# Four graph-attention layers: rows spread over the partitions by BF16 products of three parts, in place of FP32 transposes of a broadcast column

## The chip, the cores and the metric

The kernel runs on one core of a Trainium2 chip. The metric is the device time of one execution in microseconds; the figure for a kernel is the median of its runs. One further execution is taken by the hardware profiler, and all views of the profile come from that one.

## What is computed

The input `x` has 32 graphs of 512 nodes with 256 features; one adjacency matrix `adj` of 512 x 512 serves all of them. Each graph goes through four layers, each of them `x = x + gnn(relu(layernorm(x)), adj)`. The attention of a layer has this core (here layer 2; the others differ in the slope, in the mask and in the closing function):

```python
Wh = jnp.einsum('bnf,fo->bno', h, W)
s_i = Wh @ a1
s_j = Wh @ a2
e = leaky_relu(s_i[:, :, None] + s_j[:, None, :], negative_slope=0.2)
e = jnp.where(mask[None, :, :], e, -inf)
attention = softmax(e, axis=-1)
h_prime = jnp.einsum('bij,bjo->bio', attention, Wh)
return elu(h_prime)
```

Layer 0 does this with four heads of 64 features. Layer 1 has two attentions with dense layers around them: one over all pairs of nodes, with no mask and 512 features, and one with the mask. Layers 2 and 3 have one head of 256 features.

## The kernel before, in words

**Tiling.** A graph's 512 nodes lie as four tiles of 128 partitions (`NT` = 4). The loop at the end of `gat_stack` runs over the 32 graphs, called batches here, and records for each the pieces of all four layers: layer norm and transposition (`layernorm_relu_T`), products with the weights (`project`, `dense_relu_T`), attention (`gat_heads`, `full_gat_T`, `gat`), and the closing functions (`add_elu` and its like). Products are FP32 with 128 x 128 weights (`product`, L408).

**Rows.** The scores e are the sum of one number per row and one per column. A number per node comes as a column, one per partition. To add it along the free axis it must be a row, the same in all 128 partitions. The kernel makes such rows in two ways:

- `spread` (L621) makes a row of 512 in PSUM: for each of the four node tiles it broadcasts the column of 128 numbers to 128 x 128 and transposes it on TensorE in FP32 (`transposes`, L398). In the profile these are the instructions `row<-ident,...`.
- `lines` and `row_of` (L627, L641) transpose the column, copy it to SBUF, write it to DRAM as a line and read it back into all partitions by DMA (`line<-turned`, `rb<-line`).

`spread` is called 15 times per batch. `peaks` (L647) needs one row for each of the four heads and each of the three single-head attentions; from it VectorE takes the largest masked score of each node (`left`, L654). `weights_T` (L683) needs one for each of the same seven; with it VectorE makes `y` (L697), to which GpSimd adds the mask (L707, L715) and of which ScalarE takes the exponential into `pt` (L708, L722), the weights of the last product. `full_gat_T` (L827) needs one, for `ptf` (L877). The row of `tmax` in the same function is made by a transpose of its own, not by `spread`. Between the peaks and the weights, `score_columns` (L667) computes the columns u, top, ca, cb, cc, ct by tiny instructions on VectorE and GpSimd.

**Order.** Nothing is issued where it is recorded. `do` (`Plan.add`) stores each piece with its engine, a price in ns, its inputs and outputs. `Plan.order` then runs a list scheduler over all batches: up to `DEPTH` = 5 batches are open at a time, and on each engine the ready piece with the lowest key goes first. The key is the batch's number times `PERIOD` (103600 ns) minus a due time from a list: `FIRST` for the setup, `URGENCY` for a batch, the same list for each. The resulting order is fixed in the program: every engine issues its pieces in that order, and the hardware's semaphores make it wait where an input is late. Tiles come from pools with a fixed number of buffers per kind (`SLOTS`), of which the scheduler keeps account.

**Filler.** Where the schedule leaves TensorE a gap of 400 ns or more, dummy transposes (`filled`, L1017) are put in: six tenths of the gap at 110 ns each (`FILL`, `FILL_NS`, `FILL_FROM`). Their result is not used.

Of the kernel before, what the change touches and what calls it, by code (L numbers as in the profile page):

```python
# [10 lines left out]
BF16 = mybir.dt.bfloat16  # L11
# [22 lines left out]
SLOTS = {"b8": (7, 3), "b4": (14, 4), "b2": (14, 4), "b1": (10, 2), "ps": (7, 0), "tiny": (1000, 0), "dram": (12, 0)}  # L34

DEPTH = 5
PERIOD = 103600
# [7 lines left out]
    49957, 66495, 153342, 82735, 144893, 18248, 163947, 104419, 59651, 169283, 167420, 27958, 91780, 230242,  # L45
    195004, 201919, 109150, 118275, 41409, 148351, 105924, 84158, 33663, 128315, -31046, 92771, 80073,
    -45028, 28235, 136777, -16929, 40188, 120535, 69018, 81157, 34057, 45864, 64938, 93847, 22979, 32782,
    -10095, -7685, 78515, -28222, 19420, -8026, 14562, 65514, 92596, 50809, 54059, 90452, -2420, 84889,
    -14583, 182093, 91531, 6874, 128004, -23771, -69759, 210945, 103417, 96629, 177264, 97081, 141216,
    228810, 79944, 208774, 181698, 34991, 127254, 226356, -9989, 145084, 102532, 51302, 57785, 135746,  # L50
    80518, 8900, 128919, 64999, 72213, 100118, -191301, 129287, 126778, 107678, 38434, 214310, -59056,
    21096, 128569, -77796, 31871, 74871, 45424, 52264, -8376, 19505, -47500, 133347, 67984, 70285, 186177,
    -15984, 104650, 146444, -6977, 74654, 209924, -4928, 74371, 174294, 40423, 51951, 50262, 29464, 45416,
    3988, 20540, -30268, 143961, 32626, 29520, 89804, -46895, -71848, 192873, -94019, -16097, 82357,
    -169645, 44440, 58074, 23239, 29426, 38323, 69931, 62358, 28167, 54402, 35577, -76917, -57030, -27704,
    46576, -51547, -24313, -49157, 37623, -166471, -262408, -40277, -75897, 2495, -34811, -74370, 10822,
    -15615, -38619, -14324, 87924, -14732, 53506, -26615, -76490, 65133, 111389, 71959, 93636, 216417,
    118024, 163785, 26618, -73110, 16741, 9419, -10974, -26368, 86308, 35587, -14529, 9505, -23652, 31209,
    -35827, 87676, 57894, 76693, 67541, -81967, -32754, 78132, 16981, 15839, 11266, -39752, -44185, -180983,
    -106465, -45466, -89834, -11687, 103426, 151973, 157389, 186709, 237443, 270307, 278957, 17921, 218966,  # L60
    105429, 178416, 116249, 84788, 142806, 50637, 86803, 147442, 126624, 122625, -24526, 224818, 181273,
    122134, 261099, 188560, 278444, 309233, 202098, 46668, 146708, 13559, -27972, -149859, 4547, -115510,
    38885, 107791, -163000, 38869, -279727, -120416, -64868, -65585, -103808, 25837, -296121, 16410, -66665,
    -247882, -82470, -195328, -56781, -67125, -74463, -260380, -10356, -293322, -28794, -66573, -118165,
    117861, -244495, 33153, -14981, 71927, -75326, 49632, -75897, 12372, -59742, -253914, -34455, -280537,
    60459, -56427, -20405, -76842, -84804, -76638, -87008, 6362, -96566, -92921, -140211, -40235, 9737,
    1430, 138501, -8164, -11585, -790, 92727, -18209, -59964, 33770, 120062, 48291, -69971, -116178, -43376,
    -75934, -22587, -855, -7366, 64764, -21815, -173536, -191622, -247, -89468, -141561, -5472, -71333,
    -71091, -23345, -35224, -60425, -31184, -36678, -96715, -93204, -104153, 122741, -103991, -49069,
    -52273, 103915, -129888, -87436, -90017, -84147, -248017, -153179, -142134, -195377, -246140, -94749,  # L70
    -281312, -209508, -156148, -170174, -173938, -110763, -202784, -90958, -123778, -230905, -217447,
    -158358, -191908, -181567, -150880, -166302, -173285, -145335, -192412, -213127, -112164, -79463,
    -80154, -45304, -115344, -213688, -61711, -71844, -179488, -7519, -10195, -123581, -92377, -130342,
    -156089, -168165, -158280, -78069, -97410, 20095, 52768, -118896, -100859, -22248, -140758, -98924,
    -171258, -214761, -144742, -191503, -188885, -161622, -179163, -210494, -197100, -75155, -143396,
    -114654, -120868, -88478, -67661, -85469, -105261, -231208, -147545, -195786, -143928, -132751, -203479,
    -51238, -198637, -307380, -218655, -234274, -292902, -81910, -227932, -110271, -9939, -267811, -133305,
    96531, -164689, -28167, 25068, -163586, -170683, -125323, -118603, -47000, -182274, -161878, -209482,
    -210149, -168999, -138546, -191158, -233690, -133535, -231298, -285256, -155744, -125493, -243944,
    -223209, -190911, -249846, -244877, -146750, -260327, -392277, -245282, -212678, -202761, -168108,  # L80
    -206988, -163184, -234077, -225292, -151778, -418885, -146975, -166246, -197351, -165479, -253278,
    -164022, -7427, -227404, -223194, -205947, -290945, -299944, -191474, -275233, -246375, -249699,
    -253455, -249835, -216585, -256193, -283065, -390887, -270743, -284915, -267017, -418553, -281245,
    -293102, -238408, -177593, -347600, -366149, -358476, -414408, -536943, -384769, -405112, -314429,
    -370595, -265928, -543033, -409858, -416969, -320333, -443009, -407966, -431291, -243310, -493060,
    -378266, -346645, -225670, -370270, -376164, -325328, -399421, -374586, -398079, -417234, -461239,
    -465521, -400816, -409787, -543463, -345783, -366473, -257474, -479888, -496847, -470513,
]
FIRST = [
    -31437, 25750, -1105, 144955, 89002, 275880, 128415, 204208, 154195, 226450, 96820, 179479, 7870,  # L90
    -118045, 26290, 146438, 138609, 157057, 205913, -16123, 59630, 57501, -56814, 5247, -4577, -6068,
    -45189, -27458, 74268, 87671, 62434, 55789, -15727, -51036, -133151, -170623, -122434, -106956, -88821,
    -45241, -84685, -17322, -151531, 663, -157813, -74980, -174232, -62374, -58576, 11927, -19486, -48352,
    77279, -175495, -146175, -169316, -241074, -142701, -178875, -141702, -62487, -96044, -41405, -94885,
    -228054, -41409, -191710, -235324, -125187, -188700, -74514, -165891, -142656, -170202, 6399, -96844,
    -155386, -142053, -171779, -291299, -271981, -405298, -401521, -247815, -210715, -198935, -245058,
    -90055, -125151, -183656, -54990, -77623, -143327, -261274, -244716, -325695, -246171,
# [224 lines left out]
def gat_stack(  # L322
# [33 lines left out]
    small = ctx.enter_context(tc.tile_pool(name="small", bufs=7))  # L356
# [7 lines left out]
    def take(t):  # L364
        if t.kind == "ps":
            t.real = ps.tile(t.shape, t.dtype, name=t.name, tag="ps")
        elif t.kind == "dram":
            t.real = dram.tile(t.shape, t.dtype, name=t.name, tag="line%d" % t.shape[0])
        elif t.kind == "tiny":
            t.real = small.tile(t.shape, t.dtype, name=t.name)  # L370
        else:
            t.real = sized(t.kind, t.name, t.shape, t.dtype)
# [21 lines left out]
    def transposes(dst, srcs, holds=()):  # L394


        def run(o, *parts):
            return [nc.tensor.transpose(o[:, n * P : (n + 1) * P], a, ident) for n, a in enumerate(parts)]  # L398

        do(PE, 109.2 * len(srcs), [dst], srcs, run, holds)  # L400
# [21 lines left out]
    make_identity(nc, ident)  # L422
    minus1 = const.tile([P, 1], F32, name="minus1")
# [197 lines left out]
    def spread(cols, holds=()):  # L621

        row = Later("ps", "row", [P, N])
        transposes(row.all, [cols(t).view(lambda a: a.to_broadcast([P, P])) for t in range(NT)], holds)
        return row
# [21 lines left out]
    def peaks(t_col, far, peak):  # L647

        row = spread(t_col)
# [33 lines left out]
    def weights_T(ca, line_b, cc, ct, farT, even):  # L683
# [5 lines left out]
        row_a = spread(ca, [pt])  # L689
# [50 lines left out]
    def gat(srcT, wx, far, farT, lift, slope, own, finish):  # L740
# [8 lines left out]
        peaks(lambda t: v[:, t, D + 2 : D + 3], far, lambda it: peak[:, it : it + 1])  # L749
# [12 lines left out]
        ca, *cs = (lambda t, c=c: c[:, t : t + 1] for c in (ca, *cs))  # L762
        pt = weights_T(ca, (line_b, 0), *cs, farT, not own)
# [12 lines left out]
    def gat_heads(srcT, wx, far, farT, slope, finish):  # L776
# [13 lines left out]
        peak = Later("tiny", "peak_h", [P, H, NT])  # L790
        for hd in range(H):
            peaks(lambda t: st[:, 1, hd, t : t + 1], far, lambda it: peak[:, hd, it : it + 1])
# [277 lines left out]
```

## Time and profile before

| what | us |
|---|---|
| median of 3 runs (3439.34 to 3440.38) | 3439.69 |
| the profiled execution's own time | 3439.76 |
| its span, first to last instruction | 3437.8 |
| TensorE busy, weight loads aside | 3397.8 |
| VectorE busy | 2629.5 |
| ScalarE busy | 1962.7 |
| GpSimd busy | 1657.1 |

The lines of the profile are read like this. A group of instructions is named by its line in the kernel, engine and operation, then output `<-` inputs by the program's tile names, the shapes and the number of instructions; after the first bar stand the time in which at least one of the group ran and the mean duration in ns; after the second, the engine's idle time just before them and what ended it. PE is TensorE, PEld its weight loads (they overlap with PE), DVE VectorE, ACT ScalarE, POOL GpSimd, SP the engine that issues the DMAs. TensorE is pipelined: one record lasts longer than the distance to the next, so durations of neighbours overlap. An FP32 product is recorded as two instructions, an FP32 transpose as one. The timeline gives the start and the length of runs of like instructions in us from the span's start.

### The profile page before, as it was taken

Reading aid. Unit: us, or ns where it says so; the run is one execution under the profiler, and the core shown is the slowest. Engines: PE = TensorE matmul, PEld = TensorE weight load, DVE = VectorE, ACT = ScalarE, POOL = GpSimd, SP = SyncE. Lnnn points to the kernel's source line nnn. Section 1 sums busy time; section 2 is a strip of 40 time slices with the busy share of each in tenths; the row PEclk is TensorE's granted clock in tenths of the full one; section 3 lists DMA queues with packets and bytes.
Section 4 is the critical chain, followed back from the end, with each engine's and each line's share of the span. In section 5 each row is a group of like instructions: output and inputs, shape, how many; then the busy total and the mean of one; then the engine's idle time right before and its main releaser. Section 6 shows DMA issues by size and latency. Waiting matters only on the chain. (4 is left out here: it accounts for less than half of the span.)

```text
span 3437.8 us, 55266 instructions
## 1 busy us (share of the span) xinstructions
PE 3397.8 (99%) x18801; PEld 2861.4 (83%) x18801; DVE 2629.5 (76%) x8200; ACT 1962.7 (57%) x4109; POOL 1657.1 (48%) x2089
## 2 busy tenths in 40 slices
PE   7999999999999999999999999999999999999998
PEld 7788888888888888888888888888888888888887
DVE  8587877777777777777777877777878777777764
ACT  4555565565655565555566655556655655655543
POOL 3253554454544454545444545544544545544544
PEclk9999999999999999999999999999999999999999
DMA  3000110011110011110010110010110011110000
GB/s 111 19 29 14 35 38 31 17 38 32 35 38 26 22 38 32 35 38 26 22 38 29 37 38 26 22 37 29 38 38 21 27 32 35 38 32 16 32 19 28
DMA packets 77978, 110.51 MB, mean 32 GB/s; under 512 B 7169, under 2 KB 43521, under 8 KB 77697
## 3 DMA queue, kind: packets, MB, share of 16 engines
q1 hardware_dynamic: 77696, 106.98, 9.9%
q8 instruction: 150, 2.46, 0.3%
q14 instruction: 132, 1.07, 0.1%
HBM read 89.66 MB, written 17.30 MB: 31 GB/s over the span
## 5 line engine op out<-in xcount | busy, mean ns | idle before, releaser
L715 POOL TENSOR_TENSOR y<-y,farT_some 128x512 f32<-128x512 f32 x512 | 584.9, 1176 | 311.1 <-DVE y L697 308.3
L408 PE MATMUL mm<-v,pt 128*128 128x257 f32 x3072 | 704.1, 380 | 7.0 <-ACT pt L708 4.2
L697 DVE SCALAR_TENSOR_TENSOR y<-row,cc,rb 128x512 f32<-128x512 f32 x896 | 625.2, 742 | 73.1 <-DMA rb<-line 53.5
L408 PEld LDWEIGHTS mm<-v,pt 128*128 128x128 f32 x3072 | 575.5, 190 | 88.4 <-ACT pt L708 5.4
L722 ACT ACTIVATE pt<-y,ct 128x512 f32<-128x512 f32 x640 | 459.3, 719 | 291.2 <-POOL y L715 271.5
L408 PEld LDWEIGHTS mmh<-vh,pt 128*128 128x128 f32 x4096 | 483.3, 192 | 10.0 <-ACT pt L722 1.8
L408 PE MATMUL mmh<-vh,pt 128*128 128x65 f32 x4096 | 481.8, 272 | 1.4 <-DVE y L697 0.6
L408 PE MATMUL mm<-hfc,ptf 128*128 128x257 f32 (+1 forms) x2048 | 465.6, 381 | 0.5 <-DVE ptf L877 0.4
L408 PE MATMUL mm<-wfc,out1T 128*128 128x257 f32 x2048 | 464.4, 379 | 0.0
L408 PEld LDWEIGHTS mm<-wfc,out1T 128*128 128x128 f32 x2048 | 382.2, 189 | 53.6
L408 PEld LDWEIGHTS mm<-hfc,ptf 128*128 128x128 f32 x2048 | 380.8, 189 | 52.7 <-issue 2.0
L654 DVE CUSTOM_DVE_ANT_0 left<-row,far_nz 128x512 bf16<-128x512 f32 x640 | 413.9, 681 | 9.1 <-PE row L398 9.1
L707 POOL TENSOR_TENSOR y<-y,g 128x512 f32<-128x512 f32 x256 | 323.1, 1274 | 93.7 <-issue 42.9
L613 ACT ACTIVATE h<-xt,shift,rstd 128x256 f32<-128x256 f32 x512 | 277.5, 592 | 32.1 <-DVE shift L605 32.0
L598 POOL TENSOR_SCALAR rstd<-mv 128x4 f32<-128x4 f32 x128 | 34.3, 268 | 533.9 <-DVE mv L1014 356.0
L939 ACT ACTIVATE ez<-mm,rden 128x256 f32<-128x256 f32 x256 | 120.8, 472 | 238.6 <-DVE rden L1014 167.1
L408 PE MATMUL mm<-hT,w 128*128 128x512 f32 x512 | 233.2, 592 | 0.0
L654 DVE CUSTOM_DVE_ANT_0 left<-row,far_pos 128x512 bf16<-128x512 f32 x256 | 165.5, 685 | 86.5 <-PE row L398 86.5
L408 PE MATMUL mm<-out1T,wm 128*128 128x512 f32 x512 | 224.9, 592 | 0.0
L708 ACT ACTIVATE pt<-y 128x512 f32<-128x512 f32 x256 | 160.6, 628 | 82.7 <-POOL y L707 82.7
L1014 DVE BATCH_NORM_STATS2 stats<-xt 128x6 f32<-128x256 f32 x512 | 196.9, 414 | 5.6 <-DMA xt<-in_x_dram 5.2
L971 POOL TENSOR_TENSOR xt<-xt,rz 128x256 f32<-128x256 f32 x128 | 100.8, 797 | 199.7 <-ACT rz L970 196.3
(150 smaller groups left out, 5636.8 us busy)
## 6 DMA issues: line engine op xcount, KB each, us to landing
rb<-line SPq DMA_DIRECT2D x256, 256.0 KB
xt<-in_x_dram SPq DMA_DIRECT2D x32, 512.0 KB
out_dram<-xt SPq DMA_DIRECT2D x32, 512.0 KB
line<-turned SPq DMA_DIRECT2D x128, 2.0 KB
adj_sb<-in_adj_dram SPq DMA_DIRECT2D x1, 1024.0 KB
wfc<-in_L_gnn_W_fc_dram SPq DMA_DIRECT2D x2, 512.0 KB
a_row<-in_L_gnn_a_dram SPq DMA_DIRECT2D x3, 256.0 KB
a_row<-in_L_gnn_a_fc_dram SPq DMA_DIRECT2D x1, 512.0 KB
```

What stands on the lines that cost most here:

```text
L408: nc.tensor.matmul(o, lhsT=parts[k], rhs=parts[nk + k], start=(k == 0), stop=(k == nk - 1))
L598: do(POOL, 200, [rstd.all], [mv[:, :, 1]], lambda o, a: nc.gpsimd.tensor_scalar(o, a, EPS, None, ALU.add))
L613: lambda o, a, m, s: nc.scalar.activation(o, a, AF.Relu, bias=m, scale=s),
L654: return nc.vector.tensor_tensor_reduce(out=junk, in0=a, in1=far, scale=1.0, scalar=LOWEST, op0=ALU.add, op1=ALU.max, accum_out=o,)
L697: lambda o, a, c, b: nc.vector.scalar_tensor_tensor(o, a, c, b, ALU.add, ALU.max),
L707: do(POOL, 1255, [y.all], [y.all, g.all], lambda o, y, g: nc.gpsimd.tensor_tensor(o, y, g, ALU.add))
L708: do(ACT, 521, [pt[:, jt, :]], [y.all], lambda o, a: nc.scalar.activation(o, a, AF.Exp))
L715: lambda o, y, far: nc.gpsimd.tensor_tensor(o, y, far, ALU.add),
L722: lambda o, a, c: nc.scalar.activation(o, a, AF.Exp, bias=c),
L939: do(ACT, ns, [o.all], [z, scale], lambda o, a, s=scale, f=f: nc.scalar.activation(o, a, f, scale=s))
L971: do(POOL, 685, [xi], [xi, r.all], lambda o, a, b: nc.gpsimd.tensor_tensor(o, a, b, ALU.add))
L1014: made = p.run(*(r.ap() if isinstance(r, Ref) else r for r in p.args))
```

## The change

The function `spread` is gone. In its place stand two. `in_parts` splits a column of FP32 numbers (or n columns at once) into three BF16 parts whose sum is the number: cast, subtract, cast, subtract on VectorE. It transposes the 3n columns with one BF16 transpose on TensorE and copies the result, 3n x 128, to SBUF on ScalarE. `sum_row` then makes the row: for each node tile a BF16 product of 128 columns, whose weights (`pick`) are ones for the three parts wanted and zeros elsewhere, broadcast to 128 columns. Its FP32 sum in every partition is the number.

`in_parts` is called nine times per batch: twice for all four heads together (48 lines), twice for each of the three single-head attentions and once in the full one (12 lines). `sum_row` is called 15 times, where `spread` was.

The setup makes a BF16 identity and the two `pick` tiles on GpSimd. The kind b1 has 8 buffers in place of 10, tiny 6 in place of 7, a new kind tb 6. `PERIOD` is 101300, and the lists `FIRST` and `URGENCY` have new numbers throughout. The rule for the filler is as before.

```diff
-SLOTS = {"b8": (7, 3), "b4": (14, 4), "b2": (14, 4), "b1": (10, 2), "ps": (7, 0), "tiny": (1000, 0), "dram": (12, 0)}
+SLOTS = {"b8": (7, 3), "b4": (14, 4), "b2": (14, 4), "b1": (8, 2), "ps": (7, 0), "tb": (6, 1), "tiny": (1000, 0), "dram": (12, 0)}
...
-PERIOD = 103600
+PERIOD = 101300
...
-    small = ctx.enter_context(tc.tile_pool(name="small", bufs=7))
+    small = ctx.enter_context(tc.tile_pool(name="small", bufs=6))
...
+    ident_b = const.tile([P, P], BF16, name="ident_b")
+    nc.gpsimd.tensor_copy(ident_b, ident)
+    picks = {}
+    for n in (NT, H * NT):
+        pick = picks[n] = const.tile([P, n], BF16, name="pick%d" % n)
+        nc.gpsimd.tensor_tensor(pick, ident[:, :n], ident[:, n : 2 * n], ALU.add)
+        nc.gpsimd.tensor_tensor(pick, pick, ident[:, 2 * n : 3 * n], ALU.add)
...
-    def spread(cols, holds=()):
-        row = Later("ps", "row", [P, N])
-        transposes(row.all, [cols(t).view(lambda a: a.to_broadcast([P, P])) for t in range(NT)], holds)
+    def in_parts(cols, n, name):
+        parts = Later("tiny", "parts", [P, 3, n], BF16)
+        rest = Later("tiny", "rest", [P, n])
+        turned = Later("tb", "turned_" + name, [3 * n, P], BF16)
+        tr = Later("ps", "trb", [3 * n, P], BF16)
+        do(DVE, 78, [parts[:, 0]], [cols], nc.vector.tensor_copy)
+        do(DVE, 78, [rest.all], [cols, parts[:, 0]], lambda o, a, b: nc.vector.tensor_tensor(o, a, b, ALU.subtract))
+        do(DVE, 78, [parts[:, 1]], [rest.all], nc.vector.tensor_copy)
+        do(
+            DVE,
+            78,
+            [parts[:, 2]],
+            [rest.all, parts[:, 1]],
+            lambda o, a, b: nc.vector.tensor_tensor(o, a, b, ALU.subtract),
+        )
+        do(
+            PE,
+            60,
+            [tr.all],
+            [parts.all.view(lambda a: a.rearrange("p x n -> p (x n)"))],
+            lambda o, a: nc.tensor.transpose(o, a, ident_b),
+        )
+        copy(ACT, turned.all, tr.all, P)
+        return turned
+
+    def sum_row(turned, first, holds=()):
+        row = Later("ps", "rowb", [P, N])
+        pick = picks[turned.shape[0] // 3]
+        def run(o, lines):
+            return [
+                nc.tensor.matmul(
+                    o[:, t * P : (t + 1) * P],
+                    lhsT=pick[: lines.shape[0], first + t : first + t + 1].to_broadcast([lines.shape[0], P]),
+                    rhs=lines,
+                    start=True,
+                    stop=True,
+                )
+                for t in range(NT)
+            ]
+        do(PE, 58 * NT, [row.all], [turned.all], run, holds)
         return row
...
-        row = spread(t_col)
+        row = sum_row(parts, first)
...
-        row_a = spread(ca, [pt])
+        row_a = sum_row(parts_a, first, [pt])
...
-        peaks(lambda t: v[:, t, D + 2 : D + 3], far, lambda it: peak[:, it : it + 1])
+        peaks(in_parts(v[:, :, D + 2], NT, "t"), 0, far, lambda it: peak[:, it : it + 1])
...
-        pt = weights_T(ca, (line_b, 0), *cs, farT, not own)
+        pt = weights_T(in_parts(ca.all, NT, "a"), 0, (line_b, 0), *cs, farT, not own)
...
+        parts_t = in_parts(st[:, 1].view(lambda a: a.rearrange("p h t -> p (h t)")), H * NT, "th")
         for hd in range(H):
-            peaks(lambda t: st[:, 1, hd, t : t + 1], far, lambda it: peak[:, hd, it : it + 1])
+            peaks(parts_t, hd * NT, far, lambda it: peak[:, hd, it : it + 1])
...
+        parts_a = in_parts(flat[0], H * NT, "ah")
         for hd in range(H):
-            ch, *cs_h = (lambda t, c=c: c[:, hd, t : t + 1] for c in (ca, *cs))
-            pt = weights_T(ch, (line_b, hd), *cs_h, farT, False)
+            cs_h = (lambda t, c=c: c[:, hd, t : t + 1] for c in cs)
+            pt = weights_T(parts_a, hd * NT, (line_b, hd), *cs_h, farT, False)
...
-        q_row = spread(lambda t: c[:, 1, t : t + 1], [pt])
+        q_row = sum_row(in_parts(c[:, 1, :], NT, "q"), 0, [pt])
```

## The prediction

> **What bounds the kernel now.** I read the page's busy table first, then the table by stretches of time, then the groups of instructions and the timeline of TensorE, to learn what one spread of a row costs.
>
> ```profile
> span 3437.8 us, 55266 instructions
> ...
> PE 3397.8 (99%) x18801; PEld 2861.4 (83%) x18801; DVE 2629.5 (76%) x8200; ACT 1962.7 (57%) x4109; POOL 1657.1 (48%) x2089
> ```
>
> A busy share is an average, so the middle of the run is asked alone (columns: stretch, its length, busy us and instructions of PE, PEld, DVE, ACT, POOL, then clock and DMA):
>
> ```profile
> 1500.00:2500.00 1000.00, 999.49 (x5528) 845.10 (x5527) 779.73 (x2456) 587.82 (x1235) 496.05 (x621) 1.00 0.10 32
> ```
>
> TensorE lacks half a microsecond of 1000 at full clock; VectorE has 22% free, ScalarE 41%, GpSimd 50%. Busy here could still be filler[...]. The same table for the tile "filled" (PE, then PEld) says it is not:
>
> ```profile
> 0.00:100.00 100.00, 23.08 (x192) 21.70 (x192) 0.95 0.32 106
> 100.00:300.00 200.00, 0.00 (x0) 0.00 (x0) 1.00 0.06 19
> 300.00:3200.00 2900.00, 0.38 (x2) 0.25 (x2) 1.00 0.10 31
> 3200.00:3438.00 238.00, 36.02 (x303) 33.88 (x303) 0.99 0.07 21
> ```
>
> So the middle is pure TensorE work, and a batch costs what its TensorE instructions cost. The transposition of tmax comes once a batch, and two in a row show the period:
>
> ```profile
> 2033.39 0.27 PE L398 MATMUL row<-ident,tmax 128*128 128x128 f32 x1
> ...
> 2137.14 0.27 PE L398 MATMUL row<-ident,tmax 128*128 128x128 f32 x1
> ```
>
> 2137.14 - 2033.39 = 103.75 us per batch. Only the start and the end have idle time and filler. The removed instructions are these, by the groups:
>
> ```profile
> L398 PE MATMUL row<-ident,ca 128*128 128x128 f32 x896 | 132.0, 277 | 0.6 <-DVE ca L677 0.5
> ...
> L398 PE MATMUL row<-ident,st 128*128 128x128 f32 x512 | 66.6, 273 | 0.0
> ...
> L398 PE MATMUL row<-ident,v 128*128 128x128 f32 x384 | 58.3, 273 | 0.0
> ...
> L398 PE MATMUL row<-ident,c 128*128 128x128 f32 x128 | 19.2, 273 | 0.0
> ```
>
> The mean of 273 ns is latency, in which neighbours overlap; the cost is the distance from start to start:
>
> ```profile
> 613.65 1.00 PE L408 MATMUL mmh<-vh,pt 128*128 128x65 f32 x8
> 614.49 0.60 PE L398 MATMUL row<-ident,ca 128*128 128x128 f32 x4
> 614.93 1.90 PE L408 MATMUL mmh<-vh,pt 128*128 128x65 f32 x16
> 616.66 0.60 PE L398 MATMUL tr<-ident,ef 128*128 128x128 f32 x4
> ```
>
> Four transposes take 614.93 - 614.49 = 0.44 us. Over all spread records between 400 and 3200 us, start to start is 109.2 ns. The mmh products, which stream only 65 columns, still take about 0.11 us a record (1.73 us for 16)[...].
>
> [...] No instruction of the kernel before is a BF16 product[...]. [...] the same tiny subtraction ca takes 155 ns in the median and 464 ns in the mean, 1262 at most.
>
> **The change, part by part.**
>
> Removed: per batch (896 + 512 + 384 + 128) / 32 = 60 transposes of 109.2 ns, 6.55 us of TensorE, all on the path in the middle.
>
> Added on TensorE: 60 BF16 products of 128 columns, each with a weight load of its own, and 9 BF16 transposes (two for the four heads, two for each of three single-head layers, one for the full layer). [...] I take 58[...], since in this trace loads run wholly behind the products and a BF16 column is half as wide. A transpose loads only 12 or 48 columns and streams 128[...], and I take 60. Sum: 60 x 0.058 + 9 x 0.060 = 3.48 + 0.54 = 4.02 us. Saved: 6.55 - 4.02 = 2.53 us a batch, 81 us in 32.
>
> Added on VectorE: 9 x 4 = 36 tiny instructions a batch: 18 casts at some 155 ns and 18 subtractions of two SBUF inputs at 155 to 464 ns: 2.8 + 2.8 to 8.4 = 5.6 to 11.2 us. VectorE now works 0.780 x 103.75 = 80.9 us a batch and would work 86.5 to 92.1 of about 101.2. That costs nothing while this is hidden beside TensorE; if the order leaves no slack at some place, TensorE waits. Queued behind a late subtraction are VectorE's y, left and PSUM copies, and those feed GpSimd, ScalarE and then the products. I allow 0.1 us a batch, 3 us in all (below nothing is excluded: TensorE had no stall to lose).
>
> Added on ScalarE: 9 copies of the turned parts at 239 ns, 2.2 us, on 61.0 us of work: hidden. Its queue has them ahead of exps by a quarter of a microsecond each.
>
> The chain from a column to its row grows by four dependent VectorE steps of 0.2 us (u to top to cb at the end of the trace are 0.2 us apart), a transpose of 0.27 and a copy of 0.26 us, some 1.5 us with the handovers. In the middle other batches cover it. For the second rows (from ca) the DMA path through lines and row_of is longer anyway (line and rb take 1.15 and 2.98 us at the end of the trace). For the first rows (peaks) there is no such cover at the start and the end.
>
> Start and end: before, 497 fillers of 109 ns (54 us) and 3437.8 - 3397.8 = 40 us of idle, of which 10 precede the first instruction: 84 us that go with the fillers. The built order of the changed kernel has 584 fillers, 251 at the start and 333 at the end, none between. The rule that sets them, a fixed share of each long gap, is unchanged, so I scale: 84 x 584 / 497 = 99, +15 us. Bounds: 0 (the new order's gaps are only cut up differently) to 25.
>
> Moved or shrunk: PERIOD and the lists alter the order only; SP's 128 line and 256 rb transfers, and the loads and stores, are as many as before and DMA is at 10%. Fewer b1 and tiny buffers could make a VectorE write wait for an old reader; they are short-lived, so nothing, and what they may cost lies within the stall case below. Five small GpSimd instructions at setup fall into the 9.86 us in which TensorE waits for data anyway.
>
> Sum on the profiled execution (3439.76 us: the span of 3437.8 and 2.0 around it; the median is 3439.69, the same): 3439.8 - 81 + 15 + 3 = 3377 us.
>
> **Rivals.**
>
> Stalls: VectorE at 86 to 91% with long dependent chains of tiny steps lets TensorE wait about 1 us a batch, 32 us in all in place of 3: 3406. For it: the long waits on GpSimd; against: TensorE lost 0.5 us of 1000 with VectorE at 78%.
>
> [...]
>
> Slower: the new weight loads on TensorE run at the FP32 pace, so a product takes 111 ns, the change doesn't do what it says, and the nine transposes come on top: 60 x 1.8 ns + 0.54 = 0.65 us a batch, 21 us, plus 15: 3476. It decides from a product of 109.2 - 9 (transposes, 0.54 / 60) - 8 (15 us / 32 / 60) = 92 ns on. For it: mmh's pace; against: a cast to 16 bits halves the bytes of each column[...].
>
> **Chances.** The forecast (3350 to 3395) 0.68, stalls 0.12[...], slower 0.08, a time within the 0.2% (7 us, about what a measurement of this kernel tells from no change; a product near 92 ns) 0.02. So faster 0.90, same 0.02, slower 0.08. The low end takes [...] no longer start or end: 3439.8 - 87 = 3353, so 3352. The high end takes in stalls [...]: 3424. What is left out is the slower end and the tails, under 2 in 10.
>
> **What would show it.** Start to start of rowb products about 58 ns, under 0.24 us for a row of four; a period of about 101.2 us; VectorE at 86 to 91% in the middle and TensorE still above 99.5%; fillers none in the middle. Wrong if rowb pairs take 80 ns or more, if TensorE in the middle waits for parts, turned or y, or if start and end take over 25 us more.

## The result and the profile after

| | before | changed |
|---|---|---|
| median of 6 runs, us | 3439.52 | 3535.92 |
| lowest to highest | 3437.66 to 3440.85 | 3533.04 to 3537.91 |
| profiled span | 3437.8 | 3535.3 |

The ratio is 1.028, with a 95% interval from 1.0267 to 1.0294: the change makes the kernel slower by 96 us, where 63 us of gain were forecast. The profile's busy table:

```profile
span 3535.3 us, 57262 instructions
...
PE 3497.4 (99%) x19176; PEld 2762.5 (78%) x19176; DVE 2792.9 (79%) x9352; ACT 2063.2 (58%) x4397; POOL 1635.9 (46%) x2094
```

Its table by stretches, in the middle of the run:

```profile
1500.00:2500.00 1000.00, 999.63 (x5413) 782.52 (x5412) 799.47 (x2721) 598.37 (x1279) 469.23 (x609) 1.00 0.10 30
```

TensorE still counts as busy for all but 0.4 us of 1000 and the clock is full, and VectorE is at 80%, less than the forecast's 86 to 91%. So it looks as before: bound by TensorE, with no stall. The fillers, too, are at the start and the end (the 25 of the third stretch lie before 500 us):

```profile
0.00:100.00 100.00, 28.09 (x206) 24.41 (x206) 0.98 0.32 106
100.00:300.00 200.00, 2.79 (x20) 2.19 (x20) 1.00 0.06 20
300.00:3300.00 3000.00, 3.49 (x25) 2.78 (x25) 1.00 0.10 30
3300.00:3536.00 236.00, 41.94 (x333) 36.50 (x333) 0.99 0.07 21
```

Yet the period, from one tmax transposition to the next in the timeline, is longer:

```profile
2094.32 0.27 PE L404 MATMUL row<-ident,tmax 128*128 128x128 f32 x1
2201.01 0.27 PE L404 MATMUL row<-ident,tmax 128*128 128x128 f32 x1
```

2201.01 - 2094.32 = 106.69 us in place of 103.75 (the median of all periods is 106.70). 32 x 2.95 = 94 us; the rest of the span, the span less 32 periods, grew only from 117.7 to 121.1 us. All of the loss is in the steady middle, on an engine that never seems to wait. The groups that answer to the removed transposes:

```profile
L670 PE MATMUL rowb<-turned_ah,pick 48*128 48x128 bf16 x512 | 48.6, 218 | 0.8
...
L657 PE MATMUL trb<-ident_b,parts 128*12 128x128 bf16 x224 | 44.8, 221 | 2.5 <-DVE parts L650 2.1
...
L670 PE MATMUL rowb<-turned_th,pick 48*128 48x128 bf16 x512 | 40.1, 218 | 2.7 <-DVE y L753 2.7
...
L670 PE MATMUL rowb<-turned_a,pick 12*128 12x128 bf16 x384 | 37.7, 217 | 0.0
L670 PE MATMUL rowb<-turned_t,pick 12*128 12x128 bf16 x384 | 37.7, 217 | 0.1
```

(The numbers ahead of the shape are the rows and columns of the array in use.) Their latencies of 217 to 221 ns, below the 273 of the transposes before, show nothing wrong. The timeline of TensorE shows what the averages hide:

```profile
1008.16 1.03 PE L414 MATMUL mm<-wfc,out1T 128*128 128x257 f32 x4
1009.13 0.39 PE L670 MATMUL rowb<-turned_a,pick 12*128 12x128 bf16 x4
1009.45 2.00 PE L414 MATMUL mm<-wfc,out1T 128*128 128x257 f32 x8
1011.38 0.39 PE L670 MATMUL rowb<-turned_a,pick 12*128 12x128 bf16 x4
1011.71 0.24 PE L657 MATMUL trb<-ident_b,parts 128*48 128x128 bf16 x1
```

Eight FP32 records of 217 ns should take 1.74 us from 1009.45 on; the next row starts at 1011.38, 1.93 us later. The row's four products should take 0.22 us; the next FP32 product starts after 0.32. And the weight loads (PEld), which elsewhere start a whole product early (in the kernel before, between `mm<-hfc,ptf` products, the loads of a row start at 606.07 us and its first transpose at 606.29, one FP32 record of 0.22 us later):

```profile
1009.12 0.22 PEld L670 LDWEIGHTS <-pick 12*128 12x128 bf16 x4 [0.33 <-issue]
1009.45 1.60 PEld L414 LDWEIGHTS mm<-wfc,out1T 128*128 128x128 f32 x8
```

Both begin together with the product that needs them: at each border nothing is loaded ahead, and PEld stood idle for 0.33 us just before the row's loads. Over the middle of the run, medians from start to start: the last FP32 product before a row takes 310 ns in place of 216, the last BF16 one 145 in place of 56, and the first FP32 record behind it 321 in place of 216 (a transpose 165 in place of 109). That is some 94 + 89 + 105 = 288 ns for each visit to the new instructions, and a batch has 18 visits.

### The profile page after: what moved, and what is told of

Read it like the earlier page. It is cut to its first block, busy times and chain, and to the rows that moved or that the text cites. A ratio compares the mean times of both kernels' runs of the same rounds, so it can differ in the third digit from the quotient of the medians.

```text
span 3535.3 us, 57262 instructions
## 1 busy us (share of the span) xinstructions
PE 3497.4 (99%) x19176; PEld 2762.5 (78%) x19176; DVE 2792.9 (79%) x9352; ACT 2063.2 (58%) x4397; POOL 1635.9 (46%) x2094
## 4 chain that ended last, share of the span: by engine, by line
PE 94%; DVE 4%; DMA 1%; ACT 1%; POOL 0%; issue 0%; POOLq 0%; DVEq 0%; ACTq 0%; SPq 0%
PE mm L414 70%; PE mmh L414 12%; PE tr L404 6%; PE rowb L670 4%; PE trb L657 1%; DVE y L753 1%; DVE left L710 1%; PE tr L688 1%; DVE stats L1073 0%; DMA rb<-line 0%; PE filled L1076 0%; DVE parts L1073 0%; DVE xt L1008 0%; DVE ez L1007 0%; POOL y L763 0%
## 5 line engine op out<-in xcount | busy, mean ns | idle before, releaser
L753 DVE SCALAR_TENSOR_TENSOR y<-rowb,cc,rb 128x512 f32<-128x512 f32 x896 | 625.8, 738 | 20.4 <-PE rowb L670 8.4
L414 PE MATMUL mm<-wfc,out1T 128*128 128x257 f32 x2048 | 483.9, 385 | 0.0
L414 PEld LDWEIGHTS mmh<-vh,pt 128*128 128x128 f32 x4096 | 475.3, 192 | 9.6 <-ACT pt L778 0.9
L710 DVE CUSTOM_DVE_ANT_0 left<-rowb,far_nz 128x512 bf16<-128x512 f32 x640 | 413.8, 679 | 9.9 <-PE rowb L670 9.7
L1019 POOL TENSOR_TENSOR rz<-rz,res 128x256 f32<-128x256 f32 x128 | 98.2, 767 | 336.2 <-ACT rz L998 278.0
L771 POOL TENSOR_TENSOR y<-y,farT_self 128x512 f32<-128x512 f32 x128 | 145.4, 1159 | 227.2 <-DVE y L753 227.2
L414 PE MATMUL mm<-hT,w 128*128 128x512 f32 x512 | 241.2, 605 | 0.0
L1073 DVE BATCH_NORM_STATS2 stats<-xt 128x6 f32<-128x256 f32 x512 | 205.3, 412 | 5.6 <-DMA xt<-in_x_dram 4.3
L670 PEld LDWEIGHTS <-pick 48*128 48x128 bf16 (+1 forms) x1920 | 107.6, 93 | 126.7 <-issue 91.9
L710 DVE CUSTOM_DVE_ANT_0 left<-rowb,far_pos 128x512 bf16<-128x512 f32 x256 | 168.0, 683 | 48.9 <-PE rowb L670 48.8
```

What stands on the lines that cost most here:

```text
L414: nc.tensor.matmul(o, lhsT=parts[k], rhs=parts[nk + k], start=(k == 0), stop=(k == nk - 1))
L670: nc.tensor.matmul(o[:, t * P : (t + 1) * P], lhsT=pick[: lines.shape[0], first + t : first + t + 1].to_broadcast([lines.shape[0], P]), rh ...
L710: return nc.vector.tensor_tensor_reduce(out=junk, in0=a, in1=far, scale=1.0, scalar=LOWEST, op0=ALU.add, op1=ALU.max, accum_out=o,)
L753: lambda o, a, c, b: nc.vector.scalar_tensor_tensor(o, a, c, b, ALU.add, ALU.max),
L771: lambda o, y, far: nc.gpsimd.tensor_tensor(o, y, far, ALU.add),
L1019: do(POOL, 685, [r], [r, res[:, it, :]], lambda o, a, b: nc.gpsimd.tensor_tensor(o, a, b, ALU.add))
```

## The experiments

The theories, as they stood at the first runs. S: each change of TensorE from FP32 to BF16 and back costs this. R: not the type but the number of rows or columns of the array in use does. V: the visit is a symptom, and the added VectorE and ScalarE work, the longer chains or the new order cost the time.

**Pairs of instructions alone** (e1_pairs). No part of the kernel is used; TensorE gets rounds of a stretch A and a stretch B, for instance:

```diff
+        ("f_bfull", f128, 4, b128s, 4),
+        ("f_btwelve", f128, 4, b12s, 4),
...
+        ("f_ftwelve", f128, 4, f12s, 4),
+        ("f_fturn", f128, 4, t12, 1),
...
+        ("b_btwelve", b128, 8, b12s, 4),
...
+        for r in range(REPS):
+            for k in range(na):
+                a(oa, k)
+            for k in range(nb):
+                b(ob, k)
```

> The kernel leaves the whole computation out: it copies x to the output and issues sections of TensorE instructions alone, each 24 times: a stretch A (8 FP32 records of 256 columns, or 8 FP32 transposes, or 8 BF16 products), then a stretch B (4 or 16 BF16 or FP32 products of 128 columns with 12, 48 or 128 rows, or one transpose of 12 columns). Read is the time of a round over what its parts stream. Theory S (each change of TensorE from FP32 to BF16 and back lays the weight load bare): about 0.29 us a round for FP32 products with BF16 behind them, whether of 12 or 128 rows, 4 or 16 of them, or a BF16 transpose; 0.24 us where A are FP32 transposes; nothing where both are FP32 (12 rows, or a transpose of 12 columns) and nothing where both are BF16. Rival R (the change of the number of rows or columns in use does it): about 0.29 us for FP32 with FP32 of 12 rows and for BF16 with BF16 of 12 or 48 rows, nothing for FP32 with BF16 of 128 rows.

```profile
211.18 1.95 PE L46 MATMUL f_bfull_A<-xt 128*128 128x256 f32 x8
212.96 0.39 PE L46 MATMUL f_bfull_B<-xb 128*128 128x128 bf16 x4
213.18 1.51 PE L46 MATMUL f_bfull_A<-xt 128*128 128x256 f32 x6
...
262.23 1.99 PE L46 MATMUL f_btwelve_A<-xt 128*128 128x256 f32 x8
264.16 0.39 PE L46 MATMUL f_btwelve_B<-xb 12*128 12x128 bf16 x4
264.48 0.70 PE L46 MATMUL f_btwelve_A<-xt 128*128 128x256 f32 x2
...
457.16 0.27 PE L70 MATMUL f_fturn_B<-ident,xt 128*12 128x128 f32 x1
457.27 1.03 PE L46 MATMUL f_fturn_A<-xt 128*128 128x256 f32 x4
...
621.06 1.05 PE L46 MATMUL b_btwelve_A<-xb 128*128 128x256 bf16 x8
622.04 0.39 PE L46 MATMUL b_btwelve_B<-xb 12*128 12x128 bf16 x4
622.36 0.83 PE L46 MATMUL b_btwelve_A<-xb 128*128 128x256 bf16 x6
```

With all 128 rows (bfull) the row's four products take 213.18 - 212.96 = 0.22 us, as they stream; with 12 rows (btwelve) 0.32, the same 0.1 us too long as in the kernel. Median rounds, less what the parts stream (216 ns for an FP32 record of 256 columns, 109 for a BF16 product of 256 columns or an FP32 transpose, 56 for a BF16 product or transpose of 128, and for the FP32 products of B, two records of 128 columns each, the pace inside their stretch, 112 a record with few rows and 109 with few columns):

| A | B | round, ns | streams, ns | extra, ns |
|---|---|---|---|---|
| FP32 products | 4 BF16, 128 rows | 2006 | 1952 | 54 |
| FP32 products | 4 BF16, 12 rows | 2249 | 1952 | 297 |
| FP32 products | 16 BF16, 12 rows | 2919 | 2624 | 295 |
| FP32 transposes | 4 BF16, 12 rows | 1347 | 1096 | 251 |
| FP32 products | 4 FP32, 12 rows | 3007 | 2624 | 383 |
| FP32 products | 1 FP32 transpose, 12 columns | 1838 | 1837 | 1 |
| FP32 products | 1 BF16 transpose, 12 columns | 2076 | 1784 | 292 |
| BF16 products | 4 BF16, 128 rows | 1097 | 1096 | 1 |
| BF16 products | 4 BF16, 12 rows | 1304 | 1096 | 208 |
| BF16 products | 1 BF16 transpose, 12 columns | 1131 | 928 | 203 |

Theory S falls: FP32 with full BF16 pays next to nothing, and BF16 with BF16 of 12 rows pays. It is the shape. The cost is one per visit, since 16 products pay no more than 4 (295 ns against 297). One line fits neither theory: the FP32 transpose with 12 columns is free, the BF16 one is not. (In the section that alternated 12 with 48 rows the granted clock soon fell to 0.50; its few rounds before that paid 203 ns, so a change between two small tiles seems to cost as well. The other sections shown had a clock of 1.00 in the rounds that the medians come from.)

**Visits without the rest of the change** (e2_visits, and e3_control beside it). The kernel before, with one unused instruction behind each spread; the control has an FP32 transpose of the identity in its place.

```diff
+        def run(o, *parts):
+            made = [nc.tensor.transpose(o[:, n * P : (n + 1) * P], a, ident) for n, a in enumerate(parts)]
+            made.append(nc.tensor.matmul(filled, lhsT=ident_b[:12], rhs=ident_b[:12], start=True, stop=True))
+            return made
```

> The kernel before with its own order, and one unused BF16 product of 12 rows and 128 columns behind the four FP32 transposes of every spread: 15 visits to BF16 a batch, and nothing more for VectorE or ScalarE. Theory S: 15 x (0.056 + 0.24 to 0.29) = 4.4 to 5.2 us a batch, 142 to 165 us in all: 3582 to 3605 us. Rival V (the added VectorE and ScalarE work, the longer chains or the new order cost the time, and a BF16 product costs its streaming): 15 x 0.056 x 32 = 27 us: 3467 us.

> As the run with visits, but the added instruction is an FP32 transpose of 128 columns, so TensorE never leaves FP32. Both theories: 15 x 0.109 x 32 = 52 us more than before: 3492 us. It shows that an instruction put in at these places costs what it streams.

Measured: 3591.18 us with visits, 1.0442 of before (1.0427 to 1.0458), and 3485.89 with the control, 1.014 (1.0123 to 1.0157). The periods are 108.78 and 105.38 us. Per added instruction that is (108.78 - 103.75) / 15 = 335 ns for a visit that streams 56, and 109 ns for the control, just what it streams. 480 visits with no work for VectorE or ScalarE and no new order cost more than the whole change: V isn't needed.

**The change without the visits** (e4_fp32_parts). The order, the buffers, the fillers and the VectorE and ScalarE work of the change, with FP32 on TensorE:

```diff
-        parts = Later("tiny", "parts", [P, 3, n], BF16)
+        parts = Later("tiny", "parts", [P, 3, n])
...
-            lambda o, a: nc.tensor.transpose(o, a, ident_b),
+            lambda o, a: nc.tensor.transpose(o, a, ident),
...
+            return [nc.tensor.transpose(o[:, t * P : (t + 1) * P], a, ident) for t, a in enumerate(cols)]
```

> The changed kernel with its order, its buffers, its fillers and all its VectorE and ScalarE work, but TensorE stays in FP32: the parts are turned by an FP32 transpose, and the rows are made by four FP32 transposes of the broadcast column as before, at the places of the changed kernel. The turned parts are copied but not read, so the rows don't wait for them except by the order. Theory S: a batch has 60 x 0.109 + 9 x 0.109 us of this work, 0.98 more than before: 103.75 + 0.98 = 104.7 us a batch, 31 us in all, and up to 15 us at start and end: 3471 to 3486 us. Rival V: 3535 us or more, since it keeps all that V blames and has more for TensorE to stream.

Measured: 3482.01 us, 1.0124 (1.0109 to 1.014), period 104.90. V falls as the cause of the loss: the added VectorE and ScalarE work and the order are here, on a TensorE with more to stream, and the kernel is 54 us faster than the changed one. The longer chain is not here, since the rows don't read the turned parts; it is in the padded kernels below. The period is 0.17 us over the sum; 0.14 of that is a wait for VectorE, which is taken up further down. The parts' transposes have weights of 12 or 48 columns here too, in FP32, and the 0.03 us that are left leave no room for a cost at nine of them: it agrees with the odd line of the pairs.

**Which shapes pay** (e5_shapes). TensorE alone again, FP32 products with full weights as A. From here on the theory is called A: the part of the array in use changes between the whole and a smaller tile. The runs so far had 12, 48 and 128 rows and, FP32 transposes apart, 12, 48 and 128 columns; that 64 would count as a smaller tile and 96 as the whole was not shown yet.

> As the run of pairs (the computation is left out; TensorE alone, 24 rounds a section), now to find which shapes pay behind 8 FP32 records of 256 columns and full 128 x 128 weights. The run of pairs showed that BF16 of 128 rows pays nothing to speak of, and 12 rows pay whether BF16 or FP32, so the change of type is not the cause. Theory A (the part of the array in use changes between all of it and a smaller tile): products of 64 and 32 rows pay 0.29 us a round, 128 rows 0.05; 120 and 96 rows count as all of the array and pay 0.05[...]; products with weights of 12 and 64 columns pay, 96 not; BF16 transposes of 64 columns pay and of 128 not; FP32 products of 64 rows pay. Theory R (any number of rows or columns under 128): 120 and 96 rows and 96 columns pay as well.

| B | rows x columns in use | extra per round, ns |
|---|---|---|
| 4 BF16 products | 128 x 128 | 54 |
| | 120 x 128 | 56 |
| | 96 x 128 | 56 |
| | 64 x 128 | 298 |
| | 32 x 128 | 297 |
| | 128 x 96 | 54 |
| | 128 x 64 | 313 |
| | 128 x 12 | 291 |
| 4 FP32 products | 128 x 12 | 298 |
| | 64 x 128 | 385 |
| 1 BF16 transpose | 128 x 128 | 54 |
| | 128 x 64 | 313 |

Two rounds of the timeline, at 96 and at 64 rows:

```profile
265.80 1.95 PE L46 MATMUL brows_three_A<-xt 128*128 128x256 f32 x8
267.59 0.39 PE L46 MATMUL brows_three_B<-xb 96*128 96x128 bf16 x4
267.81 1.73 PE L46 MATMUL brows_three_A<-xt 128*128 128x256 f32 x7
...
316.89 1.99 PE L46 MATMUL brows_half_A<-xt 128*128 128x256 f32 x8
318.82 0.39 PE L46 MATMUL brows_half_B<-xb 64*128 64x128 bf16 x4
319.14 1.13 PE L46 MATMUL brows_half_A<-xt 128*128 128x256 f32 x4
```

At 96 rows the stretch A lasts 1.79 us to the next B, at 64 rows 1.93. The step lies between 64 and 96, as A has it; R in its first form, where all under 128 pays, falls. For the odd line the runs show no reason, but they narrow it to the columns: an FP32 transpose of 12 columns pays 1 ns, while one more section of this run, with FP32 transposes of 12 rows and all 128 columns, pays 289.

**Full visits in the kernel before** (e6_visits_full; the edit against the run with visits):

```diff
-            made.append(nc.tensor.matmul(filled, lhsT=ident_b[:12], rhs=ident_b[:12], start=True, stop=True))
+            made.append(nc.tensor.matmul(filled, lhsT=ident_b, rhs=ident_b, start=True, stop=True))
```

> As the run with visits (3591 us), but the unused BF16 product behind every spread has all 128 rows in place of 12. Theories A and R: 15 x (0.056 + 0.054) us a batch, 53 us over before: 3492 us. Theory S (the change of type costs): 3591 us again.

Measured: 3482.24 us, 1.0125 (1.011 to 1.014), period 105.18. The same 480 BF16 products at the same places, with 128 rows in place of 12: 109 us less. A visit now costs (105.18 - 103.75) / 15 = 95 ns, 39 over its streaming.

**The change with full rows, then with everything full** (e7_rows_full, e8_all_full). In the first the turned parts are put into zeroed tiles of 128 partitions; in the second the parts lie in zeroed tiles of 128 columns, so their transpose is full as well:

```diff
-                    lhsT=pick[: lines.shape[0], first + t : first + t + 1].to_broadcast([lines.shape[0], P]),
+                    lhsT=pick[:, first + t : first + t + 1].to_broadcast([P, P]),
...
-            [parts.all.view(lambda a: a.rearrange("p x n -> p (x n)"))],
-            lambda o, a: nc.tensor.transpose(o, a, ident_b),
+            [parts.all],
+            lambda o, _: nc.tensor.transpose(o, parts.full, ident_b),
```

> The changed kernel in its order, with the rows made by BF16 products of all 128 rows (the turned parts lie in tiles of 128 partitions whose other rows are zero, and so are those of the weights); the transposes of the parts still have weights of 12 or 48 columns. Theories A and R: of some 18 visits a batch the 10 that are for rows alone fall from 0.29 to 0.05 us: 106.7 - 2.3 = 104.4 us a batch, 3535 - 74 = 3461 us. Theory S: 3536 us, as the changed kernel.

> As the run before it, and the transposes of the parts have 128 columns too: the parts lie in tiles of 128 columns, zero behind the 3n that are used, two tiles for each n in place of six buffers. Theories A and R: no visit pays more than 0.05 us: 103.75 - 6.55 + 69 x 0.056 + 18 x 0.054 = 102.0 us a batch, 55 us less than before, and 3 us more at start and end as in the changed kernel: 3387 us, faster than both. Theory S: 3536 us.

Measured: 3464.27 us with full rows, 1.0075 (1.006 to 1.009), period 104.30; 3415.76 with everything full, 0.9935 (0.9919 to 0.9952), period 102.41. So 120 us of the changed kernel go by adding zeros, with the longer chain from column to row in place. Nor is it the broadcast of the weights: these full rows still use it, and the visits of 12 rows, which paid, didn't. The timeline of the second, at a transpose and a row of the heads:

```profile
1013.79 0.22 PE L672 MATMUL trb<-ident_b,parts 128*128 128x128 bf16 x1
1013.85 1.95 PE L423 MATMUL mm<-hfc,ptf 128*128 128x256 f32 x8
1015.63 0.39 PE L686 MATMUL rowb<-turned_ah,pick 128*128 128x128 bf16 x4
1015.86 1.04 PE L413 MATMUL tr<-ident,h 128*128 128x128 f32 x8
```

Eight records take 1.78 us, and the row 0.23. The expected 3387 us were missed by 29 (by 20 for the profiled execution; the four executions lie between 3407 and 3419): the period is 0.38 us over the expected one, 12 us in all, and the span less 32 periods is 7 us more than in the changed kernel. The stretches before the first tmax and behind the last are not longer than there (122.3 and 172.8 us against 122.9 and 174.3); they don't shrink with the period.

**72 of 128** (e9_72_of_128): as the run before, with 72 rows and columns, and 4 and 3 tiles for parts (the edit against that run).

```diff
+WIDE = 72
...
-        tr = Later("ps", "trb", [P, P], BF16)
+        tr = Later("ps", "trb", [WIDE, P], BF16)
...
-        few = P
+        few = WIDE
```

> The kernel of the run before, with 72 rows and columns in place of 128 everywhere in the BF16 path, and 4 and 3 tiles of parts in place of 2 and 2, since they are smaller. Theory A[...]: [...] the period of the run before, 102.4 us, and 3405 to 3416 us in all; a little less if the two buffers of parts made VectorE wait. Theory R (each size under 128 pays): 106.7 us a batch and 3536 us.

Measured: 3408.69 us, 0.991 (0.9894 to 0.9927), period 102.43. At 72 a visit costs what it does at 128, and in the run of shapes 96 and 120 rows (56 ns) and 96 columns (54 ns) paid as little as 128 (54 ns). The period is that of 128 (102.41), so the two buffers of parts had made nothing wait that counts. This is the lowest median found, 31 us under the kernel before and 127 under the changed one; from the run before it differs by 7 us in the median but not in the period.

## Why the prediction was wrong

**What bounds the kernel: right.** TensorE sets the time per batch, before and after. VectorE took the 36 tiny instructions a batch and stayed at 80% of a longer period.

**"Added on TensorE": the step that failed.** The price taken was right, in its own terms: within a run of like instructions a product takes 56 ns from start to start (57 to 73 on the average of a group), where 58 was taken. But 60 x 58 ns + 9 x 60 ns is a sum over instructions, and what costs is the border between unlike ones, for which the sum had no term. The 58 ns were an estimate of the pace inside a run, and so was the 111 ns of the slower rival; no pace there bounds a border. The step argued that "in this trace loads run wholly behind the products"; that holds in a trace whose products all use the whole array (the loads of the row at 606.29 us start 0.22 us ahead), and the change brought the first BF16 ones and the first that don't: 12 or 48 rows, or 12 or 48 columns of weights. (The FP32 transposes of cb and c have few columns too; such a transpose paid 1 ns in the pairs.) The prediction went by the pace of full tiles alone.

With the measured terms, per batch (means of 18 batches in the middle): 60 x 109.2 - 69 x 56 = 2.69 us saved; 18 borders inward and outward at 94 + 93 ns, 3.37 us; the bare first weight load, 14 x 105 ns for products of 256 columns or more and 0.16 for the other four records, 1.63; two changes between rows and transposes of parts, whose tiles differ too, at 88 and 98 ns, and 11 ns at 11 first row products, 0.31. The borders cost 5.31 us in all.

A smaller term has no border in it. Once a batch, at two rows of ah, TensorE waits for VectorE:

```profile
950.06 0.74 DVE L753 SCALAR_TENSOR_TENSOR y<-rowb,cc,rb 128x512 f32<-128x512 f32 x1
...
950.43 0.80 PE L670 MATMUL rowb<-turned_ah,pick 48*128 48x128 bf16 x8
...
950.72 0.86 DVE L968 SCALAR_TENSOR_TENSOR ef<-mm,rdenf,ef 128x256 f32<-128x256 f32 x2
950.85 0.20 PEld L670 LDWEIGHTS <-pick 48*128 48x128 bf16 x3 [0.15 <-issue]
...
951.24 0.19 PEld L414 LDWEIGHTS mm<-w3x,hT 128*128 128x128 f32 x1 [0.19 <-DVE ef L968]
951.24 0.48 PE L414 MATMUL mm<-w3x,hT 128*128 128x258 f32 x1
```

The second row starts 190 ns late at 950.85, 0.05 us after y has ended at 950.80; the product behind it starts 84 ns later than the border alone would have it, 0.05 us after the first ef. Neither y nor ef is an input of what waits, but each reads PSUM, so these look like waits for a PSUM buffer. That makes 0.27 us. Sum: 5.31 + 0.27 - 2.69 = 2.89 us, of 2.95 measured. In the version with everything full the same two waits are 0.30 and 0.17 us, and they are most of what it has over its own sum: 103.75 - 2.69 + 15 x 0.056 = 101.90, and 102.41 measured.

**"Removed": right.** 109.2 ns a transpose; the control shows that a transpose at these places is worth what it streams, 109 ns.

**VectorE, ScalarE, chains: nearly right.** They are hidden but for the 0.27 us of waits for VectorE, 9 us in all, where 0.1 a batch and 3 us were allowed. The run with FP32 parts has all their instructions and lies within the 3471 to 3486 us that TensorE's sum gave; the longer chain is in the padded kernels, with a period 4.3 us shorter than the changed one's.

**Start and end: too high.** +15 us was scaled from the fillers; +3 was measured (121.1 against 117.7).

**The rivals.** The slower one had the sign and the engine, "the new weight loads on TensorE", but the wrong mechanism: a pace of 111 ns, and a decision at 92 ns per product. The pace was 56. It gave 3476 us and 0.08. Its ground was mmh's pace in the kernel before, 112 ns in the median; that the weight loads set this pace was the author's estimate and was not shown. Stalls by VectorE exist, but at a quarter of the 1 us a batch that the rival of stalls put on them, and they are not the loss.

## What to carry to other kernels

Before TensorE work is replaced by smaller products, count the places at which the stream passes between full shapes and small ones, and charge each round trip some 0.3 us (0.20 to 0.39 in the pairs here), however many small products it holds (295 ns for 16, 297 for 4). In these runs 12, 32, 48 and 64 rows and 12, 48 and 64 columns were small, FP32 transposes of 12 columns (1 ns) apart, while 96 and 120 rows and 96 columns (54 to 56 ns), and 72 of both in the kernel (period 102.43 us against 102.41), counted as full; between 64 and 72 nothing was tried. Here 18 round trips a batch turned 2.7 us of saving into a loss. If a small product stands among full ones, pad it with zeros to a size that counted as full: in this kernel a row of four padded products took 0.22 to 0.23 us, as four small ones at 56 ns do without the border, and padding to 128 or to 72 was worth 120 or 127 us. A busy share of 99% does not show this; the distance from start to start at the borders, and a weight load that starts together with its product, do. And a small wait can hide there too: with the borders' cost gone, some 0.5 us a batch of waits for VectorE were left.

## What the runs showed of the hardware that was not expected

- The cost belongs to the shape, not to the type: 297 or 298 ns a round trip for BF16 of 12, 32 or 64 rows between FP32 products, 54 to 56 for 96, 120 or 128; with 72 in the whole kernel the period is 102.43 us, with 128 it is 102.41.
- The 54 ns that are left behind full BF16 products are the first FP32 record: 272 ns in place of 216. An estimate fits this: the FP32 load that lay bare at the borders took 105 ns, and the 56 ns of one BF16 product would cover about half of it. No run isolates it.
- FP32 transposes with 12 columns of weights don't pay (1 ns), FP32 products (298) and BF16 transposes (292) of 12 columns do, and so do FP32 transposes of 12 rows (289). No run shows why.
